# First ffn: the first choice's adapter summed in PSUM with the quarter products, the second choice's from the difference of the factors

## The chip, the cores and the metric

The kernel runs on one NeuronCore of one Trainium2 chip. It is written in Tile, a layer that orders instructions and places the semaphores by itself. Five engines work side by side: TensorE (PE; its weight loads are PEld), VectorE (DVE), ScalarE (ACT), GpSimd (POOL) and SyncE (SP, which only issues transfers here). The metric is the device time in microseconds, the median of several runs; smaller is better.

## The reference

Sixteen blocks of 128 tokens of width 512 go through two layers, each an attention and a feed-forward part (ffn), all in float32. The change is in the first layer's ffn: two of eight low-rank adapters are chosen for each token.

```
probs = softmax(x @ Wr + br);  w, idx = top_k(probs, 2)
base_h1 = x @ W1 + b1                                  # [tokens, 2048]
t1 = einsum('td,erd->ter', x, A1)                      # 8 experts, rank 16
l1 = einsum('ter,efr->tef', t1, B1) * 2.0
a  = gelu(base_h1[:, None, :] + l1)                    # per chosen expert
ca = a * combine[:, :, None];  mix = ca.sum(axis=1)
t2 = einsum('tef,erf->ter', ca, A2);  l2 = einsum('ter,edr->td', t2, B2) * 2.0
out = mix @ W2 + combine.sum(-1) * b2 + l2
```

For each token only the two chosen experts count, so the kernel makes `gelu(base + l1)` twice: once with the first choice's adapter and once with the second's.

## The kernel before

**Groups and pairs.** The first ffn runs over four groups (`g`) of 512 tokens; `lo` and `hi` are the lower and upper 256 tokens of a group. The 2048 features are 16 blocks of 128, and they are worked off in eight pairs: block `m` (near) and block `m + 8` (far). Features lie on partitions, tokens along the free dimension.

**Quarter products.** For a pair, `up_pair` (L1039) computes `x @ W1` for 2 feature blocks and 2 token halves by a Strassen scheme: seven products of quarter size, each two float32 matmuls of 128x128 weights with 256 tokens, in place of eight. The weights are sums of quarters of W1 that were made earlier and are loaded per pair into one of two slots (`load_up`, L822). The token sides are made by `quarter_tokens` (L343). The products go to four PSUM banks: `ps[0]`, `ps[1]` (named hs_ps, from a pool of two buffers that `tr_tile` hands out) and `ps[2]`, `ps[3]` (ht_ps, from the pool of four of `mm_tile`). A bank holds 512 columns, `lo` in its lower half and `hi` in its upper half. The order of the banks is 0 lo, 1 lo, 2 lo, 0 hi, 1 hi, 2 hi, 3 lo; the upper half of bank 3 is unused. Between them ScalarE copies the first product (`p1`, L1065), and VectorE adds the others up (`u2`, `u3`, `u4`, and with the bias by `biased_sum`, L1060) into two SBUF tiles of 128x512: `base` (near) and `base_f` (far).

The product of bank 1, upper half (`p5`) goes into both `base[:, hi]` (through `u4`) and `base_f[:, hi]`.

**The adapter's factors.** `spread` (L357) multiplies the tokens with all eight experts' A1 (four matmuls of 512 columns into `t_ps`, which is also a `tr_tile`), and scales it by masks of 128x512, `selT[0]` for the first choice and `selT[1]` for the second. That gives `t1[0]` and `t1[1]`, with zeros in the rows of experts that weren't chosen. The masks come from the routing (`route`) through device memory: eight transfers (`send_chosen`, L333) bring them back. `spread` is called for group 0 after the first pair's `up_pair` (L1481), and for the other groups inside the last `down` of the group before (L1509).

**Adapter, gelu and mix.** `adapt_pair` (L1080) does this for each of the pair's two blocks and each choice k, second first: one matmul of the adapter's B1 block with `t1[k]` into `l_ps` (512 columns, an `mm_tile`), an add of `base` on VectorE (L1095), and a gelu on ScalarE (L1096). The first choice's result overwrites `base`. The second's is multiplied by the ratio of the two routing weights (L1097), and GpSimd adds both into `near` or `far` (L1099) and makes the side sums for the next product (L1103 to L1105).

**Order.** The loop (L1476) issues `up_pair(m)`, then `adapt(m-1)` (L1108: eight matmul instructions of 512 columns into `t2_ps`), then `adapt_pair(m)`. Every matmul passes the helper at L164, which keeps it in the order of the program; L175 does so for transfers on SyncE's queue. The other engines' instructions are ordered by Tile's planner (except some that are pinned). Every matmul is shown at L165; in the trace a float32 matmul is two weight loads and two matmul instructions. After eight pairs, `down` (L1128) multiplies `near`, `far` and their sums, as weights, with the quarters of W2 (fy_ps).

**What stands before group 0.** In the last round of the first attention's loop (`u == last`) its output is projected by `project(v, n)` (L727): the products 1 and then 5 come last (L958, L960), and then group 0's first pair follows.

Of the kernel before, what the change touches and what calls it, by code (L numbers as in the profile page):

```python
# [11 lines left out]
ALU = mybir.AluOpType  # L12
# [3 lines left out]
P = 128  # L16
# [26 lines left out]
def kernel(  # L43
# [313 lines left out]
    def spread(q):  # L357

        g = q.g
        t_ps = tr_tile(f"t_ps{g}")  # L360
        for c in range(ND):
            matmul(
                t_ps, a1_sb[:, c, :], q.xnT[:, c, :], start=(c == 0), stop=(c == ND - 1)
            )
        q.t1 = []
        for k in range(2):
            t = fh.tile([P, GT], F32, tag=f"t1_{k}", name=f"t1_{g}_{k}")
            nc.vector.scalar_tensor_tensor(  # L368
                t, t_ps, LORA_SCALE, q.selT[k], ALU.mult, ALU.mult
            )  # L370
            q.t1.append(t)


    with tc.tile_pool(name="a0", bufs=2) as ap, tc.tile_pool(name="a0s", bufs=3) as sp:
# [501 lines left out]
        for u in range(1, last + 1):  # L876

            v = u - 1  # L880
            even, odd = 2 * u, 2 * u + 1
            if u == last:
                even = odd = None

            def soft_step(b, n, lag=1):
                if b is not None:
                    if n < 4:
                        soften(b, n)
                    if n >= lag:
                        block(b, n - lag)  # L890

            if u + 2 < last and u >= 2:
                for n in (2 * u + 4, 2 * u + 5):
                    room(n)
                    send(xs[n], x[place(n)])
            now = even
            if u == 1:
                now = odd
            else:
                gather(2 * v)  # L900
                if u < last:
                    score(even)
                if u + 1 < last:
                    if u % 2:
                        latents((u + 1) // 2)
                    turn(u + 1)
                if u < last - 1:
                    combine_next()
                elif u == last - 1:
                    turn_blocks(first)  # L910
            soft_step(now, 0)
            if u == last:
                project(v - 1, 1)
                route(first)
            project(v, 0)
            soft_step(now, 1)
            project(v, 2)
            soft_step(now, 2)
            gather(2 * v + 1)
            soft_step(now, 3)  # L920
            soft_step(now, 4)
            pair_sums(v)
            if u == last:

                right_pools.close()
                wf_pool = tc.tile_pool(name="wf", bufs=1, side="right")
                wf = wf_pool.__enter__()
                up_pools = ExitStack()
                fh = up_pools.enter_context(tc.tile_pool(name="f0h", bufs=1, side="right"))
                a1_sb = wf.tile([P, ND, E * ER], F32, name="a1_sb")  # L930
                b1_sb = wf.tile([P, FF], F32, name="b1_sb")
                a2_sb = wf.tile([P, NF, E * ER], F32, name="a2_sb")
                send(a1_sb, f_a1T.rearrange("(c p) r -> p c r", p=P))
                ring1 = wp.tile([P, 2, FF], F32, tag="w16", name="ring1")
                for m in range(2):
                    load_up(0, m)
                send(b1_sb, f_b1T)
                send(a2_sb, f_a2T.rearrange("(c p) r -> p c r", p=P))
                send_chosen(first)
                quarter_tokens(first)  # L940
            project(v, 6)
            if 1 < u < last:
                carry(even)
            if u < last - 1:
                combine_next()
            now = None
            if 1 < u < last:
                score(odd)
                now = odd
            project(v, 3)  # L950
            soft_step(now, 0)
            if u == last - 1:
                route_parts(first)
            project(v, 4)
            soft_step(now, 1)
            soft_step(now, 2)
            if u != last - 1:
                project(v, 1)  # L958
            soft_step(now, 3)
            project(v, 5)  # L960
            soft_step(now, 4)
            if u < last:
                carry(odd)
            if v < KEPT // 2:
                for n in (2 * v, 2 * v + 1):
                    send(xk[n], xs[n])
            for _ in range(0 if u >= last - 1 else 1 if u > 1 else 2):
                combine_next()
            if u % 2 == 0 and u + 2 < last:
                roped[u // 2 + 1] = rope(u // 2 + 1, kv_next)  # L970
            elif u + 3 < last:
                kv_next = load_kv((u + 3) // 2)
            if u + 2 < last:
                deviations(u + 2)
            if 1 < u and u + 1 < last:
                for p in keys_and_queries(u + 1):
                    if p == 3 and u + 2 < last:
                        normalise(u + 2)
            elif u + 2 < last:
                normalise(u + 2)  # L980

            if u == last - 2:
                first = measure(0)
                blocks(first, wp.tile([P, ND, GB, P], F32, tag="w16", name="xb_f0_0"))
# [54 lines left out]
    def up_pair(q, m):  # L1039

        g = q.g
        w = ups.pop((g, m))
        far = m + NF // 2
        bias, bias_f = bias1_sb[:, m : m + 1], bias1_sb[:, far : far + 1]


        ps = [tr_tile(f"hs_ps{g}_{m}_{n}") for n in range(2)]
        ps += [mm_tile(f"ht_ps{g}_{m}_{n}") for n in range(2)]

        def product(bank, cols, n):  # L1050
            dst = ps[bank][:, cols]
            for c in range(2):
                matmul(dst, w[:, n, c, :], q.rhs[n][:, c, :], start=c == 0, stop=c == 1)
            return dst

        def part(name):
            return fh.tile([P, half], F32, tag=name, name=f"{name}_{g}_{m}", bufs=2)

        def biased_sum(dst, product, bias, other):
            nc.vector.scalar_tensor_tensor(dst, product, bias, other, ALU.add, ALU.add)  # L1060

        base = tp.tile([P, GT], F32, tag="t", name=f"base_{g}_{m}")
        base_f = tp.tile([P, GT], F32, tag="t", name=f"base_{g}_{far}")
        p1, u2, u3, u4 = part("p1"), part("u2"), part("u3"), part("u4")
        nc.scalar.copy(p1, product(0, lo, 0))  # L1065
        biased_sum(base[:, lo], product(1, lo, 1), bias, p1)
        nc.vector.tensor_tensor(u2, product(2, lo, 4), p1, ALU.add)
        nc.vector.tensor_tensor(u3, product(0, hi, 5), u2, ALU.add)
        p5 = product(1, hi, 3)
        nc.vector.tensor_tensor(u4, p5, u2, ALU.add)  # L1070
        biased_sum(base_f[:, hi], p5, bias_f, u3)
        biased_sum(base[:, hi], product(2, hi, 6), bias, u4)
        biased_sum(base_f[:, lo], product(3, lo, 2), bias_f, u3)
        if m + 2 < NF // 2:
            load_up(g, m + 2)
        elif g + 1 < NG:
            load_up(g + 1, m + 2 - NF // 2)
        return base, base_f

    def adapt_pair(q, m, bases):  # L1080
# [8 lines left out]
        for j, base in enumerate(bases):  # L1089
            f = m + j * NF // 2  # L1090
            second = tp.tile([P, GT], F32, tag="t", name=f"a_{g}_{f}")
            for k, a in ((1, second), (0, base)):
                l_ps = mm_tile(f"l_ps{g}_{f}_{k}")
                matmul(l_ps, b1_sb[:, ts(f, P)], q.t1[k], start=True, stop=True)
                nc.vector.tensor_tensor(a, l_ps, base, ALU.add)  # L1095
                nc.scalar.activation(a, a, AF.Gelu_apprx_tanh)  # L1096
            q.mixed = nc.vector.tensor_tensor(second, second, q.ratioT, ALU.mult)  # L1097
            mix = (q.near, q.far)[j][:, m].rearrange("p h t -> p (h t)")
            nc.gpsimd.tensor_tensor(mix, base, second, ALU.add)  # L1099
            acts.append((f, (base, second)))  # L1100
# [374 lines left out]
    for g in range(NG):  # L1475
        last = g == NG - 1  # L1476
        held = None
        for m in range(NF // 2):
            bases = up_pair(q, m)
            if g == 0 and m == 0:  # L1480
                spread(q)  # L1481
            if held is not None:
                adapt(q, m - 1, held)
            held = adapt_pair(q, m, bases)
            if g > 0 and m == 3:
                for b in range((g - 1) * GB, g * GB):
                    moments1(b)
# [201 lines left out]
```

## Time and profile before

| what | value |
|---|---|
| runs | 1516.78, 1516.98, 1519.6 us; median 1516.98 |
| the profiled execution | 1517.14 us, its span 1515.4 us |
| mean granted clock of TensorE | 0.997 |
| busy in the span: PE, PEld | 1482.0 us (98%), 997.1 us (66%) |
| busy: DVE, ACT, POOL | 842.0, 432.7, 468.9 us |
| adapter matmuls l_ps in the first ffn, 512 columns | 256 instructions, 115.2 us busy |
| adds of l_ps and base, L1095, 128x512 | 64 of 687 ns and 64 of 691 ns |
| sums with bias, L1060, 128x256 from ht_ps | 64 of 482 ns |
| sum without bias, L1067, 128x256 | 32 of 424 ns |

How to read it: a line of the timeline gives start and length in us, engine, line, output and inputs by the program's tile names, shapes and the number of instructions merged; in brackets stands how long the engine had been idle before, and what ended that. The lengths of matmuls overlap, because they are pipelined; the distance from start to start is what one costs when they follow each other. The program's `t1` is named t in the trace, `selT` and `ratioT` are selT, `second` is a, and `s3` lies in the tile named ring.

### The profile page before, as it was taken

How to read it: one execution, taken by the hardware profiler on the slowest of the kernel's cores; microseconds unless marked ns; L12 is line 12 of the kernel's file. 1: busy time of each engine (PE TensorE's matmuls, PEld its weight loads, DVE VectorE, ACT ScalarE, POOL GpSimd, SP SyncE). 2: the span in 40 equal slices, each digit the busy share in tenths (PEclk: the TensorE clock that was granted, in tenths of full speed). 3: DMA queues.
4: the chain of work that ended last, by engine and by line, in shares of the span. 5: the costliest groups of instructions: out<-in, count | busy, mean ns of one | idle time of the engine just before them, and what ended most of it. 6: DMA issues, size and time to landing. Idle time of an engine off the chain costs nothing. (4 is left out here: it accounts for less than half of the span.)

```text
span 1515.4 us, 19448 instructions
## 1 busy us (share of the span) xinstructions
PE 1482.0 (98%) x6744; PEld 997.1 (66%) x6744; DVE 842.0 (56%) x1729; ACT 432.7 (29%) x1423; POOL 468.9 (31%) x485
## 2 busy tenths in 40 slices
PE   7999999999999999999999999999999899999998
PEld 5667778878877666876688667866666444444443
DVE  3264654654566555555574556465656766847422
ACT  2252432433331222012211221022123554534310
POOL 2052633632522234113330432033224333322200
PEclk9999999999999999999999999999999999999999
DMA  9435567444446611642246224622354464625302
GB/s 300 122 76 90 145 174 177 101 113 101 89 79 160 234 64 66 159 134 73 73 112 157 73 73 109 160 73 73 84 140 65 66 113 80 86 36 90 68 28 98
DMA packets 365106, 163.50 MB, mean 108 GB/s; under 512 B 291664, under 2 KB 339536, under 8 KB 362832
## 3 DMA queue, kind: packets, MB, share of 16 engines
q1 hardware_dynamic: 362176, 157.39, 41.9%
q0 software_dynamic: 1536, 3.15, 1.5%
q10 hardware_dynamic: 1296, 1.71, 0.3%
q8 instruction: 54, 0.88, 0.2%
q14 instruction: 44, 0.36, 0.1%
HBM read 106.35 MB, written 18.09 MB: 82 GB/s over the span
## 5 line engine op out<-in xcount | busy, mean ns | idle before, releaser
L1099 POOL TENSOR_TENSOR near<-base,a 128x512 f32<-128x512 f32 x32 | 42.3, 1321 | 346.6 <-ACT base L1096 192.6
L680 POOL TENSOR_TENSOR e<-e,rden_a 128x512 f32<-128x512 f32 x64 | 66.1, 1040 | 186.8 <-DVE rden_a L678 186.8
L165 PE MATMUL q_ps<-xnT_a,fq 128*128 128x256 f32 (+1 forms) x448 | 117.3, 414 | 0.3 <-DVE xnT_a L85 0.3
L165 PE MATMUL l_ps<-t,b_sb 128*128 128x512 f32 x256 | 115.2, 593 | 1.4 <-DVE t L368 1.4
L197 POOL TENSOR_TENSOR e<-e,rden_a 128x512 f32<-128x512 f32 x64 | 66.4, 1039 | 159.7 <-DVE rden_a L195 157.6
L1096 ACT ACTIVATE a<-a 128x512 f32<-128x512 f32 x64 | 40.3, 629 | 257.0 <-DVE a L1095 257.0
L673 ACT ACTIVATE e<-s_ps,nmx_a 128x128 f32<-128x128 f32 x256 | 90.2, 385 | 80.3 <-DVE nmx_a L662 39.3
L190 ACT ACTIVATE e<-e,nmx_a 128x128 f32<-128x128 f32 x256 | 98.8, 387 | 30.3 <-DVE nmx_a L185 30.3
L1095 DVE TENSOR_TENSOR a<-l_ps,base 128x512 f32<-128x512 f32 x64 | 44.0, 687 | 107.9 <-PE l_ps L165 107.9
L165 PEld LDWEIGHTS q_ps<-xnT_a,fq 128*128 128x128 f32 x448 | 85.9, 193 | 25.4 <-issue 12.5
L1161 DVE SCALAR_TENSOR_TENSOR x<-fy_ps,gw,x 128x256 f32<-128x256 f32 x112 | 46.5, 475 | 80.1 <-PE fy_ps L165 80.1
L165 PEld LDWEIGHTS l_ps<-t,b_sb 128*128 128x128 f32 x256 | 48.6, 190 | 61.6 <-issue 57.4
L165 PE MATMUL fy_ps<-ring,far 128*128 128x256 f32 x384 | 87.2, 380 | 0.0
L165 PE MATMUL y_ps<-fo_raw,c 128*128 128x256 f32 x384 | 85.8, 380 | 0.9 <-DVE c L85 0.9
L747 DVE SCALAR_TENSOR_TENSOR x<-y_ps,gates,x 128x256 f32<-128x256 f32 x112 | 48.7, 477 | 65.9 <-PE y_ps L165 65.8
L165 PEld LDWEIGHTS fy_ps<-ring,far 128*128 128x128 f32 x384 | 72.7, 190 | 13.6 <-issue 4.0
L165 PEld LDWEIGHTS y_ps<-fo_raw,c 128*128 128x128 f32 x384 | 72.4, 190 | 10.6 <-ACT c L87 1.0
L165 PE MATMUL ht_ps<-T,ring 128*128 128x256 f32 x256 | 65.7, 379 | 0.0
L165 PE MATMUL t_ps<-a,a_sb 128*128 128x512 f32 x128 | 65.4, 592 | 0.0
L165 PE MATMUL t_ps<-base,a_sb 128*128 128x512 f32 x128 | 65.4, 592 | 0.0
L165 PE MATMUL y_ps<-fo_sums,c 128*128 128x256 f32 x256 | 60.8, 386 | 1.4 <-DVE c L85 0.8
L165 PEld LDWEIGHTS hs_ps<-xnT_f,ring 128*128 128x128 f32 x256 | 48.7, 190 | 18.5 <-issue 13.4
(253 smaller groups left out, 2957.4 us busy)
## 6 DMA issues: line engine op xcount, KB each, us to landing
ring<-w SPq DMA_DIRECT2D x32, 896.0 KB, 4.5
eT<-eb SPq DMA_DIRECT2D x312, 64.0 KB, 2.3
ring<-w SPq DMA_DIRECT2D x16, 1024.0 KB, 5.9
ring<-in_f_w SPq DMA_DIRECT2D x12, 1024.0 KB, 5.5
wq<-in_wq SPq DMA_DIRECT2D x8, 512.0 KB, 5.5
quarters<-in_f_w SPq DMA_DIRECT2D x32, 128.0 KB, 2.8
w<-sums SPq DMA_DIRECT2D x8, 512.0 KB, 3.6
quarters<-in_f_w SPq DMA_DIRECT2D x16, 256.0 KB, 3.3
```

The lines of the kernel that those rows point to most:

```text
L165: ins = nc.tensor.matmul(*args, **kw)
L190: nc.scalar.activation(dst[:, ts(i, P)], src[:, ts(i, P)], AF.Exp, bias=nmx[:, i : i + 1], accum_out=den[:, i : i + 1],)
L197: nc.gpsimd.tensor_tensor(d3, d3, rden.unsqueeze(2).to_broadcast([P, 4, P]), ALU.mult)
L673: nc.scalar.activation(e[:, ts(i, P)], s_ps[:, ts(i, P)], AF.Exp, bias=nmx[:, i : i + 1], accum_out=den[:, i : i + 1],)
L680: nc.gpsimd.tensor_tensor(e3, e3, rden.unsqueeze(2).to_broadcast([P, 4, P]), ALU.mult)
L747: pin(nc.vector.scalar_tensor_tensor(dst, y_ps, gate_x[0], dst, ALU.mult, ALU.add))
L1095: nc.vector.tensor_tensor(a, l_ps, base, ALU.add)
L1096: nc.scalar.activation(a, a, AF.Gelu_apprx_tanh)
L1099: nc.gpsimd.tensor_tensor(mix, base, second, ALU.add)
L1161: nc.vector.scalar_tensor_tensor(dst, y_ps[:, ts(i, half)], q.first[:, t : t + 1], dst, ALU.mult, ALU.add,)
```

## The change

The first choice's adapter product no longer gets matmuls, a bank and adds of its own. Three of the quarter products (bank 1 lo, bank 2 hi, bank 3 lo) each feed one quarter of the result alone; into these the matmul of B1 and `t1[0]`, over 256 tokens, is accumulated as a third matmul of the same group. The fourth quarter, `base_f[:, hi]`, comes from `p5`, which is shared; its adapter product is made alone in the upper half of bank 3 (`rest`) and added to `base_f[:, hi]` by VectorE. So `base` and `base_f` hold the first choice's sum when `up_pair` ends.

The second choice's tile is then `base` plus the adapter product of `t1[1] - t1[0]`; `spread` makes this difference by one more subtraction on VectorE. `adapt_pair` has one adapter matmul and one add for each block, and then the two gelus.

As the products now need `t1[0]`, group 0's `spread` moves ahead, to between the last two projections of the attention.

```diff
@@ spread
             q.t1.append(t)
+        nc.vector.tensor_tensor(q.t1[1], q.t1[1], q.t1[0], ALU.subtract)
@@ the attention's loop
             soft_step(now, 3)
+            if u == last:
+                spread(first)
             project(v, 5)
@@ up_pair
-        def product(bank, cols, n):
+        def product(bank, cols, n, adapter=None):
             dst = ps[bank][:, cols]
             for c in range(2):
-                matmul(dst, w[:, n, c, :], q.rhs[n][:, c, :], start=c == 0, stop=c == 1)
+                matmul(
+                    dst, w[:, n, c, :], q.rhs[n][:, c, :],
+                    start=c == 0, stop=c == 1 and adapter is None,
+                )
+            if adapter is not None:
+                f, tokens = adapter
+                matmul(dst, b1_sb[:, ts(f, P)], q.t1[0][:, tokens], start=False, stop=True)
             return dst
...
-        biased_sum(base[:, lo], product(1, lo, 1), bias, p1)
+        biased_sum(base[:, lo], product(1, lo, 1, (m, lo)), bias, p1)
...
-        biased_sum(base[:, hi], product(2, hi, 6), bias, u4)
-        biased_sum(base_f[:, lo], product(3, lo, 2), bias_f, u3)
+        biased_sum(base[:, hi], product(2, hi, 6, (m, hi)), bias, u4)
+        biased_sum(base_f[:, lo], product(3, lo, 2, (far, lo)), bias_f, u3)
+        rest = ps[3][:, hi]
+        matmul(rest, b1_sb[:, ts(far, P)], q.t1[0][:, hi], start=True, stop=True)
+        nc.vector.tensor_tensor(base_f[:, hi], rest, base_f[:, hi], ALU.add)
@@ adapt_pair
-            for k, a in ((1, second), (0, base)):
-                l_ps = mm_tile(f"l_ps{g}_{f}_{k}")
-                matmul(l_ps, b1_sb[:, ts(f, P)], q.t1[k], start=True, stop=True)
-                nc.vector.tensor_tensor(a, l_ps, base, ALU.add)
+
+            l_ps = mm_tile(f"l_ps{g}_{f}")
+            matmul(l_ps, b1_sb[:, ts(f, P)], q.t1[1], start=True, stop=True)
+            nc.vector.tensor_tensor(second, l_ps, base, ALU.add)
+            for a in (second, base):
                 nc.scalar.activation(a, a, AF.Gelu_apprx_tanh)
@@ the loop over pairs
             bases = up_pair(q, m)
-            if g == 0 and m == 0:
-                spread(q)
```

## The prediction

> **What bounds the kernel now.** I read the page's first part, then the stages, then the order of time inside one step of the loop that the change edits, and last the few waits that TensorE has there.
>
> ```profile
> PE 1482.0 (98%) x6744; PEld 997.1 (66%) x6744; DVE 842.0 (56%) x1729; ACT 432.7 (29%) x1423; POOL 468.9 (31%) x485
> ```
>
> TensorE is busy 98% of the span, VectorE 56%. The Trainium skill ("Trainium Kernel Development and Optimization", on reading a trace) calls matmul busy time a bad measure, since matmuls are pipelined, and weight-load busy time a good one. By that, 66%, a third would be free for a relieved VectorE to help fill: some 30 us would be in reach. By the slots below there is none: a load of 0.19 us lies under a matmul slot of 0.43. I go by the slots. Busy time by stretch, for the second group's eight feature pairs (columns: length; then busy time and instructions of each engine; clock; DMA):
>
> ```profile
> core 0: us, PE busy (x) PEld busy (x) DVE busy (x) ACT busy (x) POOL busy (x), PEclk, DMA share, GB/s
> 660.00:755.00 95.00, 95.00 (x333) 63.03 (x332) 57.86 (x115) 23.37 (x40) 35.23 (x35) 1.00 0.25 84
> ```
>
> TensorE has no hole at all in 95 us, at full clock, while VectorE works 61% of it. From here on I count TensorE in slots, start to start. The same stretch in order of time, TensorE alone (start, length, instructions; each logical fp32 matmul is two):
>
> ```profile
> 668.73 1.89 PE L165 MATMUL hs_ps<-xnT_f,ring 128*128 128x256 f32 x8
> ...
> 674.77 1.02 PE L165 MATMUL t_ps<-base,a_sb 128*128 128x512 f32 x2
> ...
> 678.21 3.60 PE L165 MATMUL l_ps<-t,b_sb 128*128 128x512 f32 x8
> 681.64 1.89 PE L165 MATMUL hs_ps<-xnT_f,ring 128*128 128x256 f32 x8
> ```
>
> One pair is 681.64 - 668.73 = 12.91 us. Seven quarter products are 28 instructions of 256 columns in 674.77 - 668.73 = 6.04 us, so 0.2157 us each; the 16 instructions of 512 columns after them take 6.87 us, 0.4294 each. TensorE's waits between 493 and 1077 us are one line:
>
> ```profile
> PE l_ps L165 <- DVE t L368: 1.4, 1, 1.4
> ```
>
> So nothing that VectorE does in this stage holds TensorE up but that once. The stage's end is set by the sum of TensorE's slots, and whatever makes TensorE wait adds to the time in full.
>
> **The products, part by part.** Per pair, first choice: before, two adapter matmuls of 512 columns (4 instructions, 4 x 0.4294 = 1.718 us). After, three of 256 columns inside the products and one alone (8 instructions, 8 x 0.2157 = 1.726 us). The columns are the same; only 0.008 us is added per pair, 32 x 0.008 = **+0.3 us**. The second choice keeps its two matmuls. Nothing is saved on TensorE.
>
> VectorE loses two adds of 128x512 (L1095, 687 to 691 ns) and gains one of 128x256 (L1067's 424 ns stands for it): 2 x 0.69 - 0.42 = 0.96 us less per pair, 31 us in all. It lies beside TensorE's unbroken slots, so it is worth **0**.
>
> **The fourth adapter product.** It is put in the upper half of bank ps[3] right behind the product whose lower half of the same bank VectorE must still read (the sum into base_f[:, lo]). Columns don't overlap; the bank is the same. Does TensorE wait? In the first group's second pair it did, in just this situation, when the product in bank ps[1]'s upper half came before the lower half had been read (in order of time: matmuls, VectorE's read, weight loads):
>
> ```profile
> 510.58 2.03 PE L165 MATMUL hs_ps<-T,ring 128*128 128x256 f32 x8
> 510.96 0.47 DVE L1060 SCALAR_TENSOR_TENSOR base<-hs_ps,bias_sb,p 128x256 f32<-128x256 f32 x1
> ...
> 511.48 0.73 PEld L165 LDWEIGHTS hs_ps<-T,ring 128*128 128x128 f32 x4 [0.27 <-DVE base L1060]
> ```
>
> The read ends at 511.43, the load follows at 511.48, and the eight matmuls take 2.03 instead of 1.89: the slot that was due at 511.44 came at 511.58, 0.15 us behind the end of the read. The Trainium skill says the same as a rule ("PSUM — Partial Sum Buffer", section on PSUM bank collisions): semaphores guard PSUM by bank and partition quadrant, not by address. It speaks against this change, and it makes a single small row general: by addresses alone this term would be 0; by the rule it is a wait in each of 32 pairs. The other products return to a bank three products later, 2.6 us on, which is why they wait hardly ever; this one returns at once.
>
> How long is the wait? In steady pairs the last sum now reads so:
>
> ```profile
> 686.82 1.03 PE L165 MATMUL ht_ps<-T,ring 128*128 128x256 f32 x4
> 687.68 1.02 PE L165 MATMUL t_ps<-base,a_sb 128*128 128x512 f32 x2
> 687.89 0.48 DVE L1060 SCALAR_TENSOR_TENSOR base<-ht_ps,bias_sb,u 128x256 f32<-128x256 f32 x1 [0.38 <-PE ht_ps L165]
> ```
>
> The product's slots end at 687.68, the read at 688.37, 0.69 later (0.21 for the matmul to drain and be seen, 0.48 to read). VectorE was waiting for it, so its queue adds nothing. In all 32 pairs I find 0.68 or 0.69, but for two (the second pair of groups 1 and 2, at 674.77 and 835.37) where normalising work of the next group lies in between and it is 1.77. After the change the same read follows the adapter's slots. With 0.15 to restart, TensorE loses 0.68 + 0.15 = 0.83 us, and matmuls stay in program order (the helper marks each), so nothing is pulled ahead: behind the waiting load stand the previous pair's adapt matmuls (t_ps) and this pair's l_ps. 32 x 0.83 = **+26.6 us**. The two busy pairs: three products are each 0.43 longer, 1.29 in all, in which VectorE can catch up on its 1.09 lateness; between 0 and +2.2, I take **+0.5**. The small wait at 511.48 may go or stay, -0.1 to 0: **-0.1**.
>
> The add that brings the fourth product into base_f (0.42) has 3.4 us of adapt matmuls before anybody needs it: 0.
>
> **Spread goes ahead of the last projection, and the first pair.** Four logical matmuls of 512 columns (3.43 us) move; the sum of slots is the same. Spread issues no transfer, but TensorE's last projection ends 3.43 us later, and the loads queued on SyncE behind it (x<-xk waits for y_ps) start that much later; what follows them, the third pair's weights, would go out near 505.5 and is first read near 523: 0. Now the wait of 1.4 us goes: spread's scaled factors were on the path only because they were made last. In slots it is more: four matmuls from 499.48 end at 502.91, and l_ps effectively restarts 0.15 after the factors' end at 504.40, so **-1.6 us**. In its place the first pair needs factor t1[0] at its second product, and that product's bank needs t_ps released (two buffers in that pool, three tiles now in a new order). Slots: spread from 489.98 to 493.41, projection to 496.86, first product to 497.72. The factors need the selection, whose last transfer is:
>
> ```profile
> 489.55 0.30 SPq L175 DMA_DIRECT2D selT<-chosen  x1
> ```
>
> It took 5.9 us to land, at 495.5 to 495.8; two scalings of 0.65 then end near 497.0, before 497.72. The cover is 0.7 us; if VectorE takes something else first, or landing is later, each us beyond it is lost. Upper bound: factors ready only at 503.8, as in the old order; five products and three adapter slots would then follow it, some 5.3 us worse than free. I take **0**, the landing being the nearer row.
>
> The new subtraction (0.69 on VectorE, four times) is behind the factors and needed only by l_ps, 10 us on: 0.
>
> **Ends of groups.** The down product's weights are the mixed activations; the eighth feature block of the last pair is needed at its 15th instruction. Before, l_ps filled 3.43 us between; now 1.72. From the first l_ps slot: add ends 1.80, gelu 2.47, product with the ratio about 3.25, GpSimd's sum (128x512, 1.28) 4.65; the load can go 0.05 later, its slot at 4.80, due at 4.74. About 0.1 late, four times; 0 to 0.6 each; **+0.4**.
>
> **Sum.** 0.3 + 26.6 + 0.5 - 0.1 - 1.6 + 0 + 0.4 = +26.1 us. The profiled execution took 1517.14 us (span 1515.4 and 1.7 around it), 0.16 above the median of the runs, 1516.98. The forecast is the median plus 26.1: **1543.1 us**; the span would be 1541.5.
>
> **Rivals.**
> - *The fourth product doesn't wait* (not slower): guarded by address, or not ordered behind that read. Place: the load of the lone adapter matmul; price 0 instead of 26.6 and 0.5. Then 1517.0 - 1.0 = 1516.0, the same. It decides once the wait is below (3.0 + 1.0)/32 = 0.12 us a pair, 3.0 being 0.2% of the time and about what a measurement can tell from no change. For it: VectorE is idle enough. Against: the row at 511.48. 5%. If VectorE's 31 us were the gain, something would have to wait for VectorE, and no row shows it; clearly faster gets 1%.
> - *The first pair is starved:* the factors come late, up to +5.3: 1548.4. For it: 0.7 us of cover, and VectorE's order there is chosen by a planner, so the scaling may stand behind the last projection's sums and statistics. Against: the transfer's landing. 9%.
> - *VectorE reads the last product late in every pair:* a 0.68 us operation (a product with the ratio, say) is placed ahead of the read. Then half a us more in each, +16: 1559. For it: the two pairs with 1.77. Against: the other 30, and VectorE has less to do. 6%.
> - The likeliest as summed: 79%.
>
> **How the numbers follow.** Own bounds of the likeliest: wait per pair from 0.73 (restart of 0.05 alone) to 0.9, that is -3.2 to +2.2; busy pairs +1.7; group ends +2. So 1539.5 to 1549, which takes in the starved first pair and leaves out the rivals of 5 and 6%, one that clears, and thin tails. Slower by over 0.2%: 79 + 9 + 6 = 94%; same 5%; faster 1%.
>
> **What would show it.** In the profile after: a new group of weight loads for ps[3] (ht_ps from the adapter's weights) 32 times, idle some 0.8 us each with VectorE's L1060-type sum as releaser, 25 us and more together; pairs of 13.75 us instead of 12.91; no wait of l_ps for t; VectorE's busy time 30 us less; TensorE's stretch of the pairs no longer without a hole. Wrong would be a pair of 12.9 us (no bank wait), of 14.3 (a late reader), or a wait of several us in the first pair.

## The result and the profile after

The changed kernel takes 1557.08 us (median of five runs, 1556.09 to 1558.49), the kernel before 1517.76 beside it: +39.3 us, a ratio of 1.0258 (95% interval 1.0244 to 1.0272). The forecast was +26.1, with 1539.5 to 1549 as its range. The direction was right, and the largest term was right; a third of the loss was not foreseen.

The profiled execution took 1558.07 us, its span is 1556.3 (before 1515.4). The first part of its page:

```profile
PE 1498.9 (96%) x6872; PEld 1016.9 (65%) x6872; DVE 844.5 (54%) x1701; ACT 421.0 (27%) x1421; POOL 467.9 (30%) x485
```

There are 128 more matmul instructions and 28 fewer on VectorE, as the sum had it, but VectorE's busy time did not fall by 30 us: it is 844.5 where it was 842.0. TensorE's waits between 480 and 1120 us (who waited for whom; total, times, longest; the lines of the pairs), where before there was one of 1.4 us:

```profile
PE ht_ps L165 <- DVE base L1071: 21.9, 32, 4.0
PE hs_ps L165 <- ACT p L1076: 2.8, 4, 0.7
PE hs_ps L165 <- DVE base L1071: 0.5, 3, 0.2
```

The first line is the forecast one, 32 times; but one of the 32 is 4.0 us long, and the two lines below it were not in the forecast. A steady pair of the second group in order of time, from its second product to its adapt matmuls (cut to what decides):

```profile
698.63 1.27 POOL L1114 TENSOR_TENSOR near<-base,a 128x512 f32<-128x512 f32 x1 [8.64 <-DVE a L1112]
...
698.83 1.62 DVE L1112 TENSOR_TENSOR a<-a,selT 128x512 f32<-128x512 f32 x1 [0.34 <-ACT a L1111]
...
700.38 0.47 DVE L1071 SCALAR_TENSOR_TENSOR base<-hs_ps,bias_sb,p 128x256 f32<-128x256 f32 x1
...
700.90 0.73 PEld L165 LDWEIGHTS hs_ps<-T,ring 128*128 128x128 f32 x4 [0.26 <-DVE base L1071]
...
704.03 0.59 PE L165 MATMUL ht_ps<-t,b_sb 128*128 128x256 f32 x2
704.66 0.48 DVE L1071 SCALAR_TENSOR_TENSOR base<-ht_ps,bias_sb,u 128x256 f32<-128x256 f32 x1 [0.81 <-PE ht_ps L165]
705.20 0.30 PEld L165 LDWEIGHTS ht_ps<-t,b_sb 128*128 128x128 f32 x2 [0.98 <-DVE base L1071]
705.20 0.70 PE L165 MATMUL ht_ps<-t,b_sb 128*128 128x256 f32 x2 [0.58 <-DVE base L1071]
...
705.74 1.02 PE L165 MATMUL t_ps<-base,a_sb 128*128 128x512 f32 x2
```

At the end of the pair the forecast shows line by line: the last product's adapter slots end at 704.46, VectorE's read at 705.14, and the adapt matmuls come at 705.74 instead of 704.89, 0.85 us late. Further up stands what was missed: VectorE's product with the ratio takes 1.62 us beside GpSimd's sum of 1.27, where it took 0.68 before, and so the sum behind it reads the second product's bank so late that the fifth product's weights wait. In the kernel before, the second of the two products started only when GpSimd's sum was all but over:

```profile
694.47 1.27 POOL L1099 TENSOR_TENSOR near<-base,a 128x512 f32<-128x512 f32 x1 [5.96 <-ACT base L1096]
...
695.64 0.68 DVE L1097 TENSOR_TENSOR a<-a,selT 128x512 f32<-128x512 f32 x1
```

The second pair of the same group loses more. ScalarE copies the pair's first product behind the load of the gelu table and four gelus. That copy started 1.91 us behind the pair's start before (first line) and starts 3.50 us behind it now; the fourth product's weights wait for it, and then the fifth product's for VectorE's sum:

```profile
670.64 0.35 ACT L1065 COPY p<-hs_ps 128x256 f32<-128x256 f32 x1
...
685.32 0.35 ACT L1076 COPY p<-hs_ps 128x256 f32<-128x256 f32 x1
...
685.72 0.73 PEld L165 LDWEIGHTS hs_ps<-T,ring 128*128 128x128 f32 x4 [1.12 <-ACT p L1076]
...
687.01 0.73 PEld L165 LDWEIGHTS hs_ps<-T,ring 128*128 128x128 f32 x4 [0.56 <-DVE base L1071]
```

Start to start, with the pair's first product as the mark:

| stretch | before, us | after, us | difference | forecast |
|---|---|---|---|---|
| spread and group 0's first pair | 14.55 | 3.43 + 15.23 | +4.1 | -0.8 |
| four second pairs (m = 1) | 13.05, 3 x 12.91 | 15.05, 3 x 15.18 | +8.8 | +3.8 |
| first pairs of groups 1 to 3 | 2 x 9.48, 9.47 | 3 x 10.33 | +2.6 | +2.5 |
| 24 other pairs | 12.91 each | 13.89 each | +23.4 | +20.2 |
| four first stretches of down | 10.34 each | 10.37 to 10.39 | +0.2 | +0.4 |
| together | | | +39.1 | +26.1 |

The spans differ by 40.9; the other 1.8 us lie outside these stretches (0.2 ahead of them, 1.6 behind the ffn) and were not followed up.

Group 0's first pair, VectorE alone, in order of time:

```profile
501.55 0.42 DVE L1079 TENSOR_TENSOR u<-hs_ps,u 128x256 f32<-128x256 f32 x1
506.57 0.42 DVE L1010 TENSOR_TENSOR b_d<-b_sb 128x256 f32<-128x256 f32 x1 [4.60 <-DMA b_sb<-in_f_b2T]
506.91 0.42 DVE L1081 TENSOR_TENSOR u<-hs_ps,u 128x256 f32<-128x256 f32 x1
507.24 0.48 DVE L1071 SCALAR_TENSOR_TENSOR base<-hs_ps,bias_sb,u 128x256 f32<-128x256 f32 x1
507.63 0.87 DVE L1071 SCALAR_TENSOR_TENSOR base<-ht_ps,bias_sb,u 128x256 f32<-128x256 f32 x2
```

The small subtraction of two halves of B2 (`b2_d`, L1010), which nobody needs for another 150 us, waits 4.6 us for its load and holds up the pair's last four sums. The lone product was due at 504.41 and could start only behind the sum that ends at 508.50. And TensorE, after that hole, is slow (stretches; the granted clock is the number ahead of DMA's share):

```profile
504.40:508.60 4.20, 0.22 (x2) 0.04 (x1) 1.94 (x5) 0.00 (x0) 0.00 (x0) 0.95 1.02 286
508.60:512.30 3.70, 3.70 (x6) 1.99 (x7) 1.12 (x2) 0.00 (x0) 0.00 (x0) 0.59 1.11 390
```

The six matmul instructions behind the hole, 2 x 0.2157 + 4 x 0.4294 = 2.15 us at full clock, take 3.6 at 0.59 of it.

### The profile page after: what moved, and what is told of

It is laid out like the page before. It is cut to its first block, busy times and chain, and to the rows that moved or that the text cites. A ratio compares the mean times of both kernels' runs of the same rounds, so it can differ in the third digit from the quotient of the medians.

```text
span 1556.3 us, 19652 instructions
## 1 busy us (share of the span) xinstructions
PE 1498.9 (96%) x6872; PEld 1016.9 (65%) x6872; DVE 844.5 (54%) x1701; ACT 421.0 (27%) x1421; POOL 467.9 (30%) x485
## 5 line engine op out<-in xcount | busy, mean ns | idle before, releaser
L674 ACT ACTIVATE e<-s_ps,nmx_a 128x128 f32<-128x128 f32 x256 | 90.3, 384 | 80.2 <-DVE nmx_a L663 39.3
L165 PE MATMUL ht_ps<-t,b_sb 128*128 128x256 f32 x192 | 61.0, 399 | 21.9 <-DVE base L1071 21.9
L1112 DVE TENSOR_TENSOR a<-a,selT 128x512 f32<-128x512 f32 x64 | 74.0, 1156 | 13.6 <-ACT a L1111 13.6
L165 PE MATMUL hs_ps<-T,ring 128*128 128x256 f32 x256 | 64.9, 392 | 3.4 <-ACT p L1076 2.8
```

The costliest lines, as they stand in the source:

```text
L165: ins = nc.tensor.matmul(*args, **kw)
L674: nc.scalar.activation(e[:, ts(i, P)], s_ps[:, ts(i, P)], AF.Exp, bias=nmx[:, i : i + 1], accum_out=den[:, i : i + 1],)
```

## The experiments

The theory after the result: three causes. The bank that is still being read (27 us), products with the ratio that GpSimd slows (3 us and part of the second pairs), and a subtraction that waits in VectorE's queue (5 us). The rival: the contention of VectorE and GpSimd is the one cause, since VectorE's busy time is up by just what the change took off it, and the waits of the lone product only show it.

### The bank

**The lone product ahead of the last one.** Same bank, but both halves are written before either is read.

```diff
-        biased_sum(base_f[:, lo], product(3, lo, 2, (far, lo)), bias_f, u3)
         rest = ps[3][:, hi]
         matmul(rest, b1_sb[:, ts(far, P)], q.t1[0][:, hi], start=True, stop=True)
+        biased_sum(base_f[:, lo], product(3, lo, 2, (far, lo)), bias_f, u3)
         nc.vector.tensor_tensor(base_f[:, hi], rest, base_f[:, hi], ALU.add)
```

> Bank theory (the lone adapter product waits because the bank it is written to is being read): it is now issued ahead of the last product into the same bank, and both halves are read after, so nothing has to wait. 31 pairs x 0.83 us and some 5 us of the first pair go: 1557.1 - 31 = 1526 us. The weight loads' wait of 34.7 us on the sums is gone. Rival (contention: the time is lost because GpSimd's sums now slow VectorE's products with the ratio, 0.68 to 1.6 us, and VectorE is late everywhere): the wait only moves to the next product that VectorE has to read; less than 5 us are gained, 1552 us or more.

Measured: 1530.23 us, 1.0088 of before (1.0068 to 1.0109). The first pairs of groups 1 to 3 are back at 9.49, steady pairs are 13.04 us instead of 13.89, and no weight load of ht_ps waits for VectorE any more. The end of such a pair:

```profile
692.92 0.59 PE L165 MATMUL ht_ps<-t,b_sb 128*128 128x256 f32 x2
693.35 1.02 PE L165 MATMUL t_ps<-base,a_sb 128*128 128x512 f32 x2
693.55 0.48 DVE L1071 SCALAR_TENSOR_TENSOR base<-ht_ps,bias_sb,u 128x256 f32<-128x256 f32 x1 [1.24 <-PE ht_ps L165]
693.96 0.41 DVE L1087 TENSOR_TENSOR base<-ht_ps,base 128x256 f32<-128x256 f32 x1
```

TensorE goes from the adapter's slots straight into the adapt matmuls (0.43 us, two slots), and VectorE's two reads lie beside them. VectorE's products with the ratio are as slow as ever here (1.16 us in the mean), so contention is not what the 27 us were. The gain falls 4 us short of the 31 that I expected, because the first pair's share did not go: 9.84 us, but the second pair then takes 16.38. With the subtraction still in VectorE's queue (it waited 3.3 us for its load there) the stall came out one pair later: the adds, gelus and with them ScalarE's copy were late, and TensorE waited 2.8 us for that copy.

**The lone product in a bank of its own,** at its old place behind the last one.

```diff
-        rest = ps[3][:, hi]
+        rest = mm_tile(f"rest_ps{g}_{m}")[:, :half]
```

> The changed kernel with the lone adapter product in a bank of its own, issued at the same place as in the change. If only the shared bank makes it wait: the waits go as they did when it was issued ahead, 1557.1 - 27 = 1530 us, pairs of 13.05 us. If its place at the end of the pair makes it wait (VectorE's queue): 1557 us, pairs of 13.89 us.

Measured: 1530.37 us, 1.0079 (1.0065 to 1.0092), steady pairs of 13.05. So it is the shared bank, not the place. Each of these PSUM tiles fills one bank, and the wait is for a semaphore of VectorE's sum, so the runs don't tell a rule by bank from one by tile, and what the chip would do without that semaphore is not shown.

**The wait by itself.** In the kernel before, the last quarter product is put behind the one in bank 2's upper half.

```diff
-        biased_sum(base_f[:, lo], product(3, lo, 2), bias_f, u3)
+        biased_sum(base_f[:, lo], product(2, lo, 2), bias_f, u3)
```

> The kernel before with one edit: the last quarter product goes to the lower half of bank 2, right behind the product in its upper half, in place of bank 3. Bank theory: 32 waits of 0.83 us, 1517.8 + 26.6 = 1544.4 us. Rival (contention), or if an address alone counts: nothing of it is in this kernel, at most 1520 us.

Measured: 1545.85 us, 1.018 (1.0163 to 1.0197), that is +28.1 us for 32 waits, 0.85 in each steady pair (13.75 or 13.76 us instead of 12.91). TensorE's waits of this kernel for VectorE's sums in the ffn:

```profile
PE ht_ps L165 <- DVE base L1060: 18.7, 32, 0.7
```

One changed digit, no operation added, and the price of the change's largest term. The idle time shown on TensorE's own row (18.7) is less than what is lost, because the modelled end of the matmul before it reaches into the hole; the distance of the pairs' starts has all of it.

### The products with the ratio

**Order of the gelus, first try:** both second choices' gelus are written ahead of both first choices', so that VectorE's products come before GpSimd's sum.

```diff
-            for a in (second, base):
-                nc.scalar.activation(a, a, AF.Gelu_apprx_tanh)
+            seconds.append(second)
+        for a in (*seconds, *bases):
+            nc.scalar.activation(a, a, AF.Gelu_apprx_tanh)
+        for j, (base, second) in enumerate(zip(bases, seconds)):
```

> The changed kernel with both second choices' gelus ahead of both first choices', so that VectorE's products with the ratio are done before GpSimd starts its sum. Bank theory: the products fall from 1.16 us to about 0.7 in the mean, VectorE's busy time falls by some 28 us, but the lone product's waits stay; only the small waits of the fifth product (24 x 0.14 us) and part of the second pairs' (4 x 1.4 us) go: 1549 to 1554 us. Rival (contention): with the products fast again most of the 39 us comes back, 1520 to 1530 us.

Measured: 1556.81 us, 1.0251 (1.0235 to 1.0266): no change that could be told. It decides nothing about the steady pairs, because the planner put ScalarE's instructions back into the old order there, and the products beside GpSimd's sum are 1.62 us long as before. Only the second pairs got the new order, and in groups 1 to 3 they fell from 15.18 to 14.75. Against that, group 0's first pair took 16.15 in this execution instead of 15.23, most of it by the clock (last section).

**The same, tied.** In seven pairs of eight the first choices' gelus are ordered behind both second choices'.

```diff
+            elif n > 1 and m < NF // 2 - 1:
+                tc.add_manual_dep(done_a.ins, both_seconds.ins.name, ...)
```

> The changed kernel; in the first seven pairs of each group the first choices' gelus are tied behind both second choices' on ScalarE, so that both products with the ratio are done when GpSimd's sum starts. If the products are slow because GpSimd runs beside them: their mean falls from 1.16 us to about 0.75, the fifth product's wait of 0.14 us goes from 24 pairs, part of the second pairs' too: steady pair 13.75 us instead of 13.89, 1557.1 - 3.4 - 2 = 1552 us. The rival (contention makes the 39 us) expects 1530 or less. If they are slow for another reason (place, size): they stay at 1.16 us, 1557 us.

Measured: 1554.05 us, 1.0235 (1.022 to 1.025). Steady pairs are 13.77 instead of 13.89, the second pairs of groups 1 to 3 14.75 instead of 15.18, and the line of hs_ps waiting for VectorE is gone from TensorE's waits. VectorE's busy time is 820.6 us instead of 844.5. The same steady pair:

```profile
695.28 1.47 DVE L1124 TENSOR_TENSOR a<-a,selT 128x512 f32<-128x512 f32 x2
...
696.62 1.27 POOL L1126 TENSOR_TENSOR near<-base,a 128x512 f32<-128x512 f32 x1 [8.89 <-ACT base L1112]
...
697.41 0.48 DVE L1071 SCALAR_TENSOR_TENSOR base<-hs_ps,bias_sb,p 128x256 f32<-128x256 f32 x1 [0.66 <-ACT p L1076]
```

Two products in 1.47 us, both begun before GpSimd starts at 696.62, and the sum behind them waits for ScalarE and no more for them. So the slow product is one that starts while GpSimd's sum already runs: the Trainium skill ("SBUF — State Buffer", on the shared port pair) says that a VectorE operation with two SBUF inputs and a GpSimd operation lock each other out: the one that starts first holds the ports for its whole instruction. The numbers fit: in the changed kernel the product started at 698.83, GpSimd's sum ended at 699.90, and 699.90 + 0.68 = 700.58 against the measured 700.45. VectorE's sums that read PSUM kept their 0.48 us beside GpSimd. What it cost is 24 x 0.12 + 4 x 0.43, some 4.6 us by the pairs (3.0 by the medians), not 39: the rival falls.

### The subtraction in the queue

**The move of spread alone,** in the kernel before.

```diff
+            if u == last:
+                spread(first)
             project(v, 5)
...
-            if g == 0 and m == 0:
-                spread(q)
```

> The kernel before with spread alone moved ahead of the last projection. As the prediction had it (the move costs nothing and the wait for the factors goes): 1517.8 - 1.6 = 1516.2 us. If the move is what makes the first pair late (the load of b2_sb goes out 3.4 us later, and the subtraction that waits for it now stands in VectorE's queue ahead of three of the first pair's sums): the wait shows at an adapter matmul that needs the bank those sums read, some 3 us, so 1517.8 - 1.6 + 3.3 = 1519.5 us, and more if the clock falls.

Measured: 1520.63 us, 1.002 (1.001 to 1.0031), slower by 3 us where the forecast's part had -1.6. In its first pair:

```profile
506.73 0.42 DVE L1009 TENSOR_TENSOR b_d<-b_sb 128x256 f32<-128x256 f32 x1 [4.45 <-DMA b_sb<-in_f_b2T]
507.07 0.48 DVE L1062 SCALAR_TENSOR_TENSOR base<-hs_ps,bias_sb,u 128x256 f32<-128x256 f32 x1
507.47 0.86 DVE L1062 SCALAR_TENSOR_TENSOR base<-ht_ps,bias_sb,u 128x256 f32<-128x256 f32 x2
507.99 0.36 PEld L165 LDWEIGHTS l_ps<-t,b_sb 128*128 128x128 f32 x2 [3.89 <-DVE base L1062]
507.99 3.64 PE L165 MATMUL l_ps<-t,b_sb 128*128 128x512 f32 x4 [3.06 <-DVE base L1062]
```

The same wait without any lone product: the third adapter matmul takes over a bank that the held-up sums have not read. And the four instructions behind the hole take 3.43 us start to start, twice their 1.72, though the hole was only 3.1 us.

**The subtraction later, first try:** written after the fourth pair.

```diff
-    nc.vector.tensor_tensor(b2_d, b2_sb[:, : D // 2], b2_sb[:, D // 2 :], ALU.subtract)
...
             held = adapt_pair(q, m, bases)
+            if g == 0 and m == 3:
+                nc.vector.tensor_tensor(b2_d, ...)
```

> The changed kernel with the small subtraction b2_d issued after the fourth pair instead of ahead of the loop, so that it can't stand in VectorE's queue in the first pair while its load has not landed. If that subtraction is what holds the first pair up (wait of 4.25 us in place of 0.83, and some 1.45 us of matmuls at the lower clock behind it): 1557.1 - 4.9 = 1552.2 us, first pair 10.3 us instead of 15.2. If the first pair is late for the factors or the moved loads themselves: no change.

Measured: 1558.53 us, 1.027 (1.0255 to 1.0286), first pair 15.20. It decides nothing: the planner put it at the same place, ahead of the fourth sum, and it waited for its load 4.60 us as before.

**The same, tied** behind the fourth pair's product with the ratio.

```diff
+                late_d = nc.vector.tensor_tensor(b2_d, ...)
+                tc.add_manual_dep(late_d.ins, q.mixed.ins.name, ...)
```

> The changed kernel with the subtraction b2_d tied behind the fourth pair's product with the ratio on VectorE. If its place in VectorE's queue holds up the first pair: first pair 10.4 us instead of 15.2 (the lone product's wait 0.83 instead of 4.25, no stretch at the lower clock), 1557.1 - 4.9 = 1552.2 us. If the first pair is late for anything else that the moved loads bring: 1557 us.

Measured: 1554.24 us, 1.0244 (1.0231 to 1.0257). The first pair is 10.33 us instead of 15.23, and the longest wait of the lone product 0.6 instead of 4.0. That is 4.9 us, as expected. The medians gained 2.8 us, the profiled spans 4.9; the runs of one kernel scatter by 2 to 5 us, so the pair's length shows the cause better than the total. Of the gain 0.9 us is lost again to a fifth pair of 14.75, into which the tied subtraction now falls.

### All of it together

**The three repairs in one kernel** (the lone product ahead, the gelus and the subtraction tied).

> The changed kernel with the lone product ahead of the last one, the gelus tied and b2_d tied behind. If the three causes are all: the first pair 9.6 us, steady pairs 12.92 us, at most 1.3 us left in each second pair, and the former wait for the factors gone: 1517.8 - 1.6 + 0.3 + 0.4, plus 0 to 5 for the second pairs, 1517 to 1522 us. If another loss is hidden behind these: above 1524 us.

Measured: 1523.14 us, 1.0035 (1.0021 to 1.0049). That is a little above the range expected, and below the 1524 that would have meant another loss. Steady pairs are 12.92, the second pairs 13.9, group 0's first pair 11.19 where 9.6 was expected, its fifth 13.30. TensorE's waits:

```profile
PE hs_ps L165 <- ACT p L1075: 2.9, 4, 0.7
PE hs_ps L165 <- DVE t L368: 1.4, 1, 1.4
```

The first line is one second pair in each group: the copy of its first product stands on ScalarE behind the table for gelu and four gelus. The second is the first pair waiting for the factors; in this execution the masks' last transfer went out at 493.26 us, 3.7 later than before, and the cover of 0.7 us was gone.

**The copy on VectorE in the second pairs:**

```diff
-        nc.scalar.copy(p1, product(0, lo, 0))
+        if m == 1:
+            nc.vector.tensor_copy(p1, product(0, lo, 0))
+        else:
+            nc.scalar.copy(p1, product(0, lo, 0))
```

> The three repairs together, and in each group's second pair the copy of the first product is made on VectorE instead of ScalarE. If the second pairs are late because that copy stands on ScalarE behind the load of the gelu table (1.28 us) and four gelus: they fall from 13.9 to 12.92 us, 1523.1 - 4 = 1519 us. If they are late because VectorE is: they stay at 13.9 us, 1523 us.

Measured: 1518.8 us, 1.0006 (0.9997 to 1.0015): the same as before. The second pairs of groups 1 to 3 fell from 13.9 to 12.95, which settles what was left of them. The first pair had its 9.49 us in this execution, but group 0's second pair took 14.46, waiting 1.3 us for a product with the ratio.

**And the masks' transfers first:**

```diff
                 send(a1_sb, f_a1T.rearrange("(c p) r -> p c r", p=P))
+                send_chosen(first)
...
-                send_chosen(first)
                 quarter_tokens(first)
```

> As the one with the copy on VectorE, and the eight transfers of the masks go out ahead of the loads of the pair weights, B1 and A2 instead of behind them. If a late landing of the masks cost the first pair 1.4 us: first pair 9.5 us, 1519 - 1.6 = 1517.4 us, within 0.2% of before; 1516 at best, since all that the change can save TensorE is the old wait of 1.6 us. If the weights, which now start later, are late in their place: 1519 us or more.

Measured: 1519.4 us, 1.0003 (0.9995 to 1.0012), the same as before, and not the 1517.4 expected. The factors were done at 495.3 us, early enough, but the first pair took 10.45: it now waits 0.7 us for one of VectorE's sums. The old wait of 1.6 us is gone in all of these, and another of 0.7 to 1.4 us stands in its place in one of group 0's first two pairs; its cause was not followed further. No version beats the kernel before.

## Why the prediction was wrong

- **What bounds the kernel: right.** TensorE's slots set the pairs; the matmul work of the repaired version is what it was (12.92 against 12.91 us a pair), and with VectorE busy 818.4 us there instead of 842.0, none of these 24 us came back as time.
- **The fourth adapter product: right, mechanism and size.** 0.83 us was forecast, 0.85 measured, by the change itself, by the two ways to remove it (13.89 to 13.05), and alone in the kernel before.
- **"It lies beside TensorE's unbroken slots, so it is worth 0": the size of a thing next to it failed.** That VectorE would be relieved by 0.96 us a pair was the sum of durations taken from the old order. The change also took 1.72 us of matmuls from between the last adds and the next pair. The second product, which used to start when GpSimd's first sum was all but over, was now ready just after that sum had begun, and it went from 0.68 to 1.62 us in every pair. VectorE's busy time rose by 2.5 us instead of falling by 31, and its sum for the second product came late: +0.12 to 0.14 us in each steady pair, 3.3 us in all, that I had put at 0.
- **"The two busy pairs: between 0 and +2.2, I take +0.5": mis-sized and for the wrong reason.** I looked at VectorE's normalising in the second pairs; VectorE had caught up on that (its last read waits for the product there). What was late was ScalarE's copy behind gelus and their table, whose cover (the 3.43 us of l_ps) the change had halved, and then the sum behind the slow product. The second pairs lost 1.2 us (group 0) and 1.4 us each beyond the bank's wait, +5.4 where I had 0.4 (the 0.5 and the -0.1 of the small wait). Of the 1.4, 0.43 went with the tied gelus and 0.95 with the copy on VectorE.
- **"The loads queued on SyncE behind it start that much later ... 0": the step that failed outright.** I followed the pair weights down the queue and left out b2_sb, which has a reader on VectorE. The load went out at 501.01 instead of 497.38 us, and the planner, in the new order, put its reader ahead of four sums of the first pair. Measured: a wait of 4.2 us instead of 0.83, and 1.45 us more for matmuls at the lower clock, +4.9 together. This is the rival "the first pair is starved" in its price (5.3), though by another operation than the factors; those were in time in the changed kernel, at 497.0 as worked out.
- **The wait for the factors: right.** It is gone (-1.6); what replaced it was more.

The sum, from the table's differences: 26.1 + 3.3 (slow products) + 5.0 (second pairs) + 4.9 (first pair), less 0.2 at the groups' ends, is 39.1; the medians differ by 39.3. The range was too narrow because its bounds were drawn around the wait alone: each cover that the change used up was priced as if the others stayed.

## What to carry to other kernels

In such a program a PSUM bank counts as a whole: a matmul into its free half waits while the other half is read, 0.85 us here each time; write both halves before either is read, or take another bank. When matmuls are moved from between a chain of small operations and its consumer, the chain's cover goes with them, so lay the chain out anew, with what now runs beside what. And a moved step delays every load queued behind it: look for each load's first reader on an in-order engine, however late its result is needed.

## What the runs showed of the hardware

A hole of 2 to 4 us in TensorE's work could halve its clock for 3.41 us behind it. With the lone product in its own bank the hole was 2.58 us (506.85 to 509.43); TensorE's busy time and the granted clock (the number ahead of DMA's share) were:

```profile
505.54:508.95 3.41, 1.31 (x5) 0.43 (x3) 1.11 (x4) 0.00 (x0) 0.00 (x0) 1.00 1.02 314
508.95:512.36 3.41, 2.92 (x5) 1.71 (x6) 2.44 (x6) 1.55 (x2) 0.00 (x0) 0.50 1.10 381
```

With spread moved alone (3.06 us) it was 0.53 over 3.4 us, with the change itself (4.0 us) 0.59. But with the lone product ahead of the last one a hole of 2.78 us (509.40 to 512.18) cost no clock at all:

```profile
507.24:510.65 3.41, 2.16 (x10) 1.55 (x9) 1.95 (x5) 2.25 (x3) 0.00 (x0) 1.00 1.10 381
510.65:514.06 3.41, 1.74 (x7) 1.24 (x8) 2.95 (x5) 1.47 (x4) 2.80 (x3) 1.00 1.03 385
```

So the length of the hole does not decide alone. In each trace of this case the halvings start a whole number of steps of 3.413 us behind the first one: in the changed kernel at 95.19, 508.20, 1235.24 and 1399.08 us, which is 121, 334 and 382 steps on. On that grid 2.1 us of the hole of 2.58 lie in one step, and the next step is halved; the hole of 2.78 is parted by a step's end into 1.25 and 1.53 us. The kernel before has both kinds as well: a hole of 2.03 us within one step, from 92.10 on, is followed by half the clock, and one of 2.44 us, from 1322.73 on, parted into two of 1.22, is not. Where in the grid a hole falls is chance here: in the first try with the gelus' order a hole of 3.84 us reached over a step's end and cost two halved steps, 0.7 of the 0.9 us by which the first pair was longer there. Waits of 0.85 us in every pair never halved it. The Trainium skill ("TensorE: Matmul & The Clock Gate", on the clock gate) puts the danger at idle gaps above some 3.4 us; here 2 us within one step were enough. A halved step adds up to 1.7 us to a single wait, which no sum of durations contains.
